# Layer 0 of a four-layer network: head values in 31 orthonormal coordinates with the denominator as the 32nd column, and the causal mask as a product on GpSimd

## The chip, the cores and the metric

The kernel runs on one core of one Trainium2 chip. Times are device microseconds of one execution of the whole program, all four layers. A core has five engines that run their own instruction queues side by side and wait for one another through semaphores: TensorE (PE, matrix products, with its weight loads shown apart as PEld), VectorE (DVE), ScalarE (ACT), GpSimd (POOL), and SyncE (SP), which here only issues DMAs. Matrix products end in PSUM, which is used here in eight banks of 128 lanes by 512 words; the other tiles lie in SBUF.

## The reference, cut to what matters

The network has four layers, each of the form x + layer(group_norm(x)). Only layer 0 is touched. It works on 16 images of 192 channels and 32 x 32 pixels, read as 1024 tokens. Its core is an mLSTM with 12 heads of 32 dimensions:

```
def step(carry, inp):
    ...
    C_new = f_s[..., None] * Cst + i_s[..., None] * (vt[..., :, None] * kt[..., None, :])
    n_new = f_s * nst + i_s * kt
    denom = jnp.maximum(jnp.abs(jnp.einsum('bhd,bhd->bh', n_new, qt)), 1.0)[..., None]
    h = jnp.einsum('bhde,bhe->bhd', C_new, qt) / denom
...
mu = hs.mean(-1, keepdims=True)
var = hs.var(-1, keepdims=True)
hn = ((hs - mu) / jnp.sqrt(var + 1e-05)).reshape(bsz, s, INNER) * mh_w + mh_b
h_out = (hn + skip * x_act) * jax.nn.silu(z)
return seq + (h_out @ w_down + b_down)
```

The result of that block and silu(seq @ w_lin + b_lin) are added, and a 3 x 3 convolution, a batch norm and a leaky ReLU follow. In the kernel the scan is done in chunks of 128 tokens: inside a chunk every token looks at the earlier ones through a matrix of scores, and a state per head carries what lies before the chunk.

One identity matters for the change. A head's output is normalized over its 32 dimensions, so its mean is taken away at once, and what is left lies in a space of 31 dimensions. With numerator u (mean already removed) and denominator e, the normalized head is u / sqrt(mean(u^2) + 1e-5 * max(e^2, 1)); the division by the denominator never has to be made.

## The kernel before

**Stages of an image.** `layer0` (line 153 on) handles one image at a time in `image(b, conv)`: image 0 first, then images 1 to 15 in a device loop (line 735) whose end is a barrier over all engines (`L735` in the profile). An image has three stages.

- *Head:* group norm, channel norm, the projections to `x_in` and the gate `sz`, a short causal convolution to `xact`, the gates and their running sums, the projections `qT` and `kT`, and `qs`, the queries scaled by the state's decay (six matmuls of `L547` whose results are multiplied on VectorE by `L551`, one PSUM bank each).
- *Chunks:* eight chunks of 128 tokens. Twelve calls of `scores(n)` each make the score tiles for two pairs (chunk, group of four heads); `turned(c)` turns a chunk's values and keys so that tokens lie on the lanes; `finish(c)` makes a chunk's outputs and updates the state.
- *Tail:* `w_lin` and `w_down`, the sum with the input copy `xr`, and the writes into the padded image `ypad`, from which the 3 x 3 convolution reads.

The convolution of image b - 1 is a generator, `conv3`, of 45 steps of one tap each (three PSUM passes of 15 taps, each pass ended by ScalarE's copy `yo`, `L392`). `fill(n)` draws n steps from it and puts them between other TensorE work. In image 0 there is nothing to draw from. In the chunk stage the order of instructions on each engine is the order of the program (`tc.manual_schedule()`); elsewhere a scheduler orders them, and it may place matmuls of the tail between the last chunks.

**The lines the change touches.**

- `scores`: for each of four PSUM banks a matmul of the identity with `mask` in bfloat16 (`L608`) first writes 0 or -1e30; then the gate exponents are added (`itg`, `at`), and beside them the products of keys and queries are made (both `L613`). ScalarE takes the exponential of the first half (`L619`), VectorE multiplies it with the second (`L622`), which gives `D`.
- `turned`: values times `cent` (`L584`), a matrix that takes away each head's mean, copied by ScalarE to `va` (`L588`) with 33 columns a head, the last of which is 1; keys transposed (`L592`) and copied to `kt`; the weighted values `vw` on GpSimd (`L596`).
- `finish`: into one PSUM bank `nd` go the numerators of three groups of four heads (`L632` from the chunk, `L645` from the state `cst`) and, as a fourth block of columns, the denominators (`L638` with `onec`, which picks a row by its place, and `L650` with `nst`, the state's denominator column). Each of these is 12 small matmuls, 32 output lanes each, four of them beside one another in the array. ScalarE squares both; GpSimd takes the maximum for the denominator (`L659`); the state is updated; two convolution taps follow; then a matmul with `mean32` (`L680`) and three with `dsel` (`L682`) make variance plus floor on every lane. Ln and Exp (`L683`, `L684`) give its inverse root, VectorE multiplies it to the numerators (`L685`), scales by `mh_w` and adds the skip path (`L687`, three times), and GpSimd multiplies by the gate into `hT` (`L691`).
- PSUM: `misc()` hands out two banks in turn, for `turned`, for the state's update and for the norm. `ps()`, used in head and tail, goes round these two and the four score banks. `nd` has one bank, the convolution another.
- Tail: outputs are 192 channels, done as two blocks of 128 lanes, the second with its 64 channels doubled (the weights hold these columns twice), so that both halves of the lanes of `ypad`'s second part get all pixels. Per block and half image two matmuls with `w_lin` and three with `w_down`, 20 in all; ScalarE applies Silu, which needs another function table than Ln and Exp.

An fp32 matmul appears in the trace as two records, so x24 stands for 12 matmuls; a transpose and the bfloat16 product appear as one.

Of the kernel before, what the change touches and what calls it, by code (L numbers as in the profile page):

```python
# [20 lines left out]
L = H * W  # L21
# [131 lines left out]
def layer0(tc, cx, NB, ydram, sdram, w1d):  # L153
    nc, I = cx.nc, cx.I
    with ExitStack() as ctx:
# [43 lines left out]
        mh_w, mh_b = (vec(nm, 128, nc.scalar) for nm in ("mh_w", "mh_b"))  # L199
# [18 lines left out]
        mask = wp.tile([128, 2 * CH], BF16, name="mask")  # L218
        identb = wp.tile([128, 128], BF16, name="identb")
        nc.vector.tensor_copy(identb, cx.ident)  # L220
# [9 lines left out]
        dsel = wp.tile([128, 3, 128], F32, name="dsel")  # L230
        idj = cx.ident.rearrange("p (j r) -> p r j", r=32)
        rowr = wp.tile([128, 3], F32, name="rowr")
        nc.vector.tensor_reduce(rowr, idj[:, 0:3, :], AX.X, ALU.add)
        for g in range(3):
            nc.vector.tensor_scalar(dsel[:, g, :], blk, rowr[:, g : g + 1], None, op0=ALU.mult)
# [12 lines left out]

        onec = wp.tile([128, 34], F32, name="onec")
        nc.vector.memset(onec, 0.0)  # L250
        nc.vector.memset(onec[:, 2:3], 1.0)
# [15 lines left out]
        mean32 = wp.tile([128, 128], F32, name="mean32")  # L267
        nc.vector.tensor_scalar(mean32, blk, 1.0 / DH, None, op0=ALU.mult)
        cent = wp.tile([128, 128], F32, name="cent")
        nc.vector.tensor_sub(cent, cx.ident, mean32)  # L270
# [6 lines left out]

        nc.vector.tensor_copy(
# [44 lines left out]
        w_down = wp.tile([128, 3, 256], F32, name="w_down")  # L323
        w_lin = wp.tile([P6, 2, 256], F32, name="w_lin")
        for t, nm, p in ((w_down, "w_down", 128), (w_lin, "w_lin", P6)):
            nc.sync.dma_start(t[:, :, 0:C], I[nm].rearrange("(k p) o -> p k o", p=p))
            nc.sync.dma_start(t[:, :, C:], I[nm][:, 128:C].rearrange("(k p) o -> p k o", p=p))
# [22 lines left out]
        for i in range(2):  # L350
            t = wp.tile([128, NH, HW1], F32, name="va%d" % i)
            nc.gpsimd.memset(t, 1.0)
            vas.append(t)

        nst = wp.tile([128, 3, DH], F32, name="nst")
        nc.gpsimd.memset(nst, 0.0)
# [44 lines left out]
        def image(b, conv):  # L401
# [166 lines left out]
            cst = big.tile([128, 3, HW1], F32, name="cst")  # L568
# [3 lines left out]
            to_den = slice(INNER, INNER + CH)  # L572
# [5 lines left out]
            def turned(c):  # L578


                cs = slice(c * CH, (c + 1) * CH)
                va, p = vas[c % 2], misc()
                for g in range(3):
                    nc.tensor.matmul(  # L584
                        p[:, groups3[g]], lhsT=x_in[:, g, 3 + c * CH : 3 + (c + 1) * CH], rhs=cent,
                        start=True, stop=True,
                    )
                nc.scalar.copy(va[:, :, 0:DH], p[:, 0:INNER].rearrange("p (h d) -> p h d", d=DH))  # L588
                if c < NCH - 1:
                    p = misc()  # L590
                    for g in range(3):
# [3 lines left out]
                    vw = wk2.tile([128, NH, HW1], F32, tag="vw", name="vw")  # L595
                    nc.gpsimd.tensor_mul(  # L596
                        vw, va, gtok[:, c].unsqueeze(2).to_broadcast([128, NH, HW1]),
# [3 lines left out]
            def scores(n):  # L601
# [5 lines left out]
                for j in range(4):  # L607
                    nc.tensor.matmul(S[j][:, two], lhsT=identb, rhs=mask, start=True, stop=False)  # L608
                for l_, r_, o in ((itg, at, 0), (kT, qT, 2)):
                    for i, (c, g) in enumerate(todo):  # L610
                        cs = slice(c * CH, (c + 1) * CH)
                        for j, r in enumerate(blocks4):
                            nc.tensor.matmul(  # L613
                                S[j][:, (o + i) * CH : (o + i + 1) * CH], lhsT=l_[r, g, cs],
                                rhs=r_[r, cs] if o == 0 else r_[r, g, cs], start=False, stop=(o == 2 and i == 1),
                            )
                for j in range(4):
                    d = wk2.tile([128, 2 * CH], F32, tag="D", name="D", bufs=12)
# [3 lines left out]
                    nc.vector.tensor_mul(d, d, S[j][:, 2 * CH :])  # L622

            def finish(c):


                cs = slice(c * CH, (c + 1) * CH)
                va = vas[c % 2]
                nd = psn.tile([128, HL], F32, name="nd")
                for g in range(3):  # L630
                    for j, r in enumerate(blocks4):
                        nc.tensor.matmul(  # L632
                            nd[r, groups3[g]], lhsT=va[:, 4 * g + j, 0:DH], rhs=D[c, g, j],
                            start=(g == 0), stop=False,
                        )
# [1367 lines left out]
```

## Time and profile before

| What | Value |
|---|---|
| median of three runs | 15609.16 us (15584.52 to 15626.19) |
| the profiled execution, its own time | 15591.93 us |
| span from its first to its last instruction | 15590.1 us |
| mean granted TensorE clock | 0.838 |
| layer 0, from the start to 3335 us | 21% of the span |
| 209.8 to 3269 us: PE, DVE, ACT, POOL busy of 3059 us | 2935, 1326, 1166, 272 us |
| the same, granted TensorE clock | 0.98 |
| 3335 to 15590 us: PE, DVE, ACT, POOL busy of 12,255 us | 9456, 10,877, 8013, 9563 us |

The profile is one execution, taken by the hardware profiler. A line of the timeline gives start and length in us, engine, source line, operation, output <- inputs, shape and count; in brackets stands the idle time of the engine before it and the instruction that ended it. The granted clock is the share of full speed at which the clock of TensorE was let through. A row of the stage table gives the busy time of each engine in a stretch with its instructions in brackets. Matmuls overlap in the array and their ends are modelled, so the distance between two starts says more than a length. In layers 1 to 3 VectorE and GpSimd are the busy engines; in layer 0 it is TensorE.

### The profile page before, as it was taken

The page shows a single profiled execution, that of the slowest core. Times are in us where ns is not written, and L with a number is a line of the kernel's source. Part 1 is how long each engine was busy: PE and PEld are TensorE (multiplying, and loading weights), DVE is VectorE, ACT ScalarE, POOL GpSimd, SP SyncE. Part 2 cuts the span into 40 slices and gives each one's busy share as a digit, 9 for nine tenths or more (in the row PEclk, how much of TensorE's full clock was granted, in tenths as well). Part 3 has the DMA queues.
Part 4 walks back from the last instruction along what each step waited for, and adds up shares of the span by engine and source line. Part 5 has one row for each costly group of instructions (what it writes and reads, how often), then busy time and mean ns, then how long its engine had stood idle before and what let it go on. Part 6 is the DMA issues. An engine that isn't in the chain of part 4 may idle for free. (4 is left out here: it accounts for less than half of the span.)

```text
span 15590.1 us, 196674 instructions
## 1 busy us (share of the span) xinstructions
PE 12621.5 (81%) x72384; PEld 5045.6 (32%) x72384; DVE 12310.8 (79%) x10295; ACT 9263.9 (59%) x12084; POOL 9861.8 (63%) x5787
## 2 busy tenths in 40 slices
PE   9999999987787777877787777877787777878755
PEld 5555555542222222222222222222222222222212
DVE  4444444448988999999989898898989898988997
ACT  3333333326666666666666666666666666666665
POOL 1000000006787878787878787878878787878785
PEclk9999999997787888878788888887888887878766
DMA  1000000017777787878787878787777787777775
GB/s 29 12 15 14 15 14 15 15 40 189 201 195 200 188 207 188 210 182 214 182 211 183 213 184 211 183 210 189 202 194 198 194 202 195 199 195 193 201 182 129
DMA packets 852126, 2412.70 MB, mean 155 GB/s; under 512 B 114352, under 2 KB 234240, under 8 KB 843520
## 3 DMA queue, kind: packets, MB, share of 16 engines
q1 hardware_dynamic: 838496, 2397.64, 60.2%
q8 instruction: 580, 9.50, 0.3%
q10 hardware_dynamic: 12704, 2.72, 0.1%
q14 instruction: 346, 2.83, 0.1%
HBM read 2018.92 MB, written 364.30 MB: 153 GB/s over the span
## 5 line engine op out<-in xcount | busy, mean ns | idle before, releaser
L1863 POOL TENSOR_TENSOR hc<-h,cb 128x1024 f32<-128x1024 f32 x3072 | 7247.3, 2371 | 2046.2 <-DVE h L1851 1557.8
L1851 DVE TENSOR_TENSOR_SCAN h<-dA,xt 128x1024 f32<-128x1024 f32 x3072 | 6912.8, 2273 | 297.0 <-POOL hc L1863 289.1
L1842 DVE TENSOR_TENSOR xt<-xt,bb 128x1024 f32<-128x1024 f32 x3072 | 3633.4, 1227 | 852.7 <-ACT xt L1831 718.9
L1835 ACT ACTIVATE dA<-dl,A 128x1024 f32<-128x1024 f32 x3072 | 3506.7, 1146 | 801.2 <-DMA dl<-dld 672.8
L1893 PE MATMUL acc<-hc,sel 128*32 128x256 f32 x24576 | 2406.8, 473 | 1707.6 <-POOL hc L1863 1705.0
L782 PE MATMUL mm<-pad,dg 128*128 128x512 f32 (+1 forms) x5580 | 2899.3, 655 | 13.3 <-ACT pad L782 9.9
L1831 ACT COPY xt<-du 128x1024 f32<-128x1024 f32 x1536 | 1557.6, 1014 | 1361.7 <-DVE h L1851 1183.5
L1893 PEld LDWEIGHTS acc<-hc,sel 128*32 128x32 f32 x24576 | 562.2, 120 | 4055.4 <-POOL hc L1863 2897.2
L782 PEld LDWEIGHTS mm<-pad,dg 128*128 128x128 f32 (+1 forms) x5580 | 995.5, 192 | 1479.2 <-issue 1363.3
L596 POOL TENSOR_TENSOR vw<-va,gtok 128x396 f32<-128x396 f32 x112 | 95.2, 850 | 1712.0 <-ACT va L588 1712.0
L782 PE MATMUL mm<-x,wgt 96*128 96x512 f32 (+1 forms) x1664 | 1064.5, 775 | 140.1 <-ACT o L782 50.0
L1884 PE MATMUL acc<-y,ident 128*128 128x512 f32 x576 | 445.7, 866 | 445.5 <-ACT y L1903 444.5
L782 POOL TENSOR_TENSOR t<-x 96x768 f32<-96x768 f32 (+4 forms) x510 | 647.5, 1290 | 204.6 <-PE mm L782 204.2
L691 POOL TENSOR_TENSOR x_in<-x_in,sz 128x384 f32<-128x384 f32 x128 | 116.8, 913 | 750.5 <-DVE x_in L687 676.7
L782 PE MATMUL mm<-d,xT 128*96 128x256 f32 x2048 | 569.1, 416 | 5.6 <-ACT o L782 5.3
L782 PEld LDWEIGHTS mm<-x,wgt 96*128 96x128 f32 (+1 forms) x1664 | 342.1, 226 | 669.9 <-issue 364.5
L782 POOL TENSOR_TENSOR duh<-dlh,xx 128x512 f32<-128x512 f32 x384 | 537.5, 1400 | 30.1
L782 POOL TENSOR_TENSOR dlh<-dlh,e 128x512 f32<-128x512 f32 x384 | 488.4, 1272 | 103.1 <-ACT e L782 101.2
L782 PE MATMUL mm<-xd,dtw 12*128 12x512 f32 x768 | 534.5, 782 | 10.0 <-ACT z L782 10.0
L622 DVE TENSOR_TENSOR D<-D,s 128x256 f32<-128x256 f32 x768 | 270.8, 415 | 322.6 <-ACT D L619 322.6
L389 PE MATMUL pc<-ypad,w_c 128*64 128x512 f32 (+1 forms) x1152 | 442.9, 633 | 80.4 <-PEq L735 41.3
L619 ACT ACTIVATE D<-s 128x256 f32<-128x256 f32 x768 | 232.7, 390 | 426.3 <-PE s L613 426.3
(331 smaller groups left out, 15374.9 us busy)
## 6 DMA issues: line engine op xcount, KB each, us to landing
dl<-dld SPq DMA_DIRECT2D x1536, 512.0 KB
du<-dud SPq DMA_DIRECT2D x1536, 512.0 KB
dld<-dlh SPq DMA_DIRECT2D x384, 256.0 KB
dud<-duh SPq DMA_DIRECT2D x384, 256.0 KB
bb<-xdr SPq DMA_DIRECT2D x128, 512.0 KB
cb<-xdr SPq DMA_DIRECT2D x128, 512.0 KB
dg<-dqd SPq DMA_DIRECT2D x270, 192.0 KB
zd<-z SPq DMA_DIRECT2D x48, 512.0 KB
```

The lines of the kernel that those rows point to most:

```text
L389: nc.tensor.matmul(p[r, :], lhsT=w_, rhs=v, start=(n == 0), stop=(n == 14))
L619: nc.scalar.activation(d, S[j][:, two], AF.Exp)
L622: nc.vector.tensor_mul(d, d, S[j][:, 2 * CH :])
L691: nc.gpsimd.tensor_mul(hT[:, :, cs], hT[:, :, cs], sz[:, :, cs])
L782: return f(out, *args, **kw)
L1831: self.nc.scalar.copy(self.xt[n], self.du[n])
L1835: self.nc.scalar.activation(self.dA[u % 3], self.dl[n % 2], AF.Exp, scale=self.A[:, blk, n : n + 1])
L1842: self.nc.vector.tensor_mul(self.xt[(n + 1 + blk) % 2], self.xt[n % 2], self.bb[blk])
L1851: nc.vector.tensor_tensor_scan(*views, 0.0, op0=ALU.mult, op1=ALU.add)
L1863: self.nc.gpsimd.tensor_mul(*views)
L1884: nc.tensor.matmul(acc, lhsT=self.cx.ident, rhs=self.y[:, g, half(pair)], start=True, stop=False)
L1893: nc.tensor.matmul(self.acc[rows4(q), q4(s)], lhsT=self.sel[:, m, :], rhs=self.hc[u % 3][:, q4(q)], start=False, stop=(s + m + blk == 3),)
```

## The change

The values of a head are no longer centred but turned into 31 orthonormal coordinates of the space without the mean (`to31`, a Helmert matrix per head, whose 32nd column is zero). The 32nd column of `va` is left at 1, so that numerator and denominator come out of one set of matmuls, and `cst` carries both. `onec`, `nst`, `dsel` and their matmuls go. A VectorE instruction raises the square of row 31 to at least 1 (`last` is 1 there and 0 elsewhere), and `norm32` weighs the coordinates with 1/32 and row 31 with 1e-5. A new step `leave(c)`, called one iteration later, goes back to channels with `back` (the transposed matrix times `mh_w`), adds the skip path from PSUM and applies the gate. The mask becomes a tile of ones and zeros in fp32 that GpSimd multiplies to `D`, after VectorE has capped the exponential at 2 in the instruction that multiplies it with the keys' products. `D` gets 14 buffers in place of 12.

In the tail the second block of channels is made once, its two half images side by side in the two halves of the lanes; two DMAs in a new function `both()`, at the start of the next iteration, copy each half to the other lanes of `ypad`. Taps are drawn in other places: `fill(2)` where `fill(3)` stood, and one and eight steps ahead of the last two `leave` calls.

```diff
-        mask = wp.tile([128, 2 * CH], BF16, name="mask")
...
+        mask = wp.tile([128, 2 * CH], F32, name="mask")
...
             def scores(n):
...
-                for j in range(4):
-                    nc.tensor.matmul(S[j][:, two], lhsT=identb, rhs=mask, start=True, stop=False)
...
-                    d = wk2.tile([128, 2 * CH], F32, tag="D", name="D", bufs=12)
+                    d = wk2.tile([128, 2 * CH], F32, tag="D", name="D", bufs=14)
...
-                    nc.vector.tensor_mul(d, d, S[j][:, 2 * CH :])
+                    nc.vector.scalar_tensor_tensor(
+                        d, d, 2.0, S[j][:, 2 * CH :], op0=ALU.min, op1=ALU.mult
+                    )
+                    nc.gpsimd.tensor_mul(d, d, mask)
...
             def finish(c):
...
-                for g in range(3):
-                    for j, r in enumerate(blocks4):
-                        nc.tensor.matmul(
-                            nd[r, to_den], lhsT=onec[:, 2 - g : 34 - g], rhs=D[c, g, j],
-                            start=False, stop=(c == 0 and g == 2),
-                        )
...
-                    for g in range(3):
-                        for r in blocks4:
-                            nc.tensor.matmul(
-                                nd[r, to_den], lhsT=nst[r, g, :], rhs=qs[r, g, cs], start=False, stop=(g == 2)
-                            )
...
-                nc.scalar.activation(h2, nd[:, 0:INNER], AF.Square)
-                dd = wk2.tile([128, CH], F32, tag="dd", name="dd")
-                nc.scalar.activation(dd, nd[:, to_den], AF.Square, scale=1e-5**0.5)
-                nc.gpsimd.tensor_scalar(dd, dd, 1e-5, None, op0=ALU.max)
+                nc.scalar.activation(h2, nd, AF.Square)
+                nc.vector.tensor_scalar(h2, h2, last, None, op0=ALU.max)
...
                 fill(2)
-                p = misc()
-                nc.tensor.matmul(p[:, 0:INNER], lhsT=mean32, rhs=h2, start=True, stop=False)
-                for g in range(3):
-                    nc.tensor.matmul(p[:, groups3[g]], lhsT=dsel[:, g, :], rhs=dd, start=False, stop=(g == 2))
...
+                p = misc()[:, 0:INNER]
+                nc.tensor.matmul(p, lhsT=norm32, rhs=h2, start=True, stop=True)
+                nc.scalar.activation(h2, p, AF.Ln)
+                nc.scalar.activation(h2, h2, AF.Exp, scale=-0.5)
+                nc.vector.tensor_mul(h2, h2, nd)
+                normed.append((c, h2))
+
+            def leave():
+
+                c, h2 = normed.pop()
+                cs = slice(c * CH, (c + 1) * CH)
+                p = misc()[:, 0:INNER]
                 for g in range(3):
-                    nc.vector.scalar_tensor_tensor(
-                        hT[:, g, cs], h2[:, groups3[g]], mh_w[:, g : g + 1], xact[:, g, cs],
-                        op0=ALU.mult, op1=ALU.add,
-                    )
+                    nc.tensor.matmul(
+                        p[:, groups3[g]], lhsT=back[:, g, :], rhs=h2[:, groups3[g]], start=True, stop=True
+                    )
+                nc.vector.tensor_add(hT[:, :, cs], xact[:, :, cs], p.rearrange("p (g t) -> p g t", g=3))
                 nc.gpsimd.tensor_mul(hT[:, :, cs], hT[:, :, cs], sz[:, :, cs])
...
                         turned(begun)
                         begun += 1
+                    if normed:
+                        leave()
...
                     else:
-                        fill(3)
+                        fill(2)
+                fill(1)
+                leave()
                 finish(ready)
+                fill(8)
+                leave()
...
+            for n in range(3):
+                e = n // 2
+                parts = [(n, slice(0, 128), slice(0, 128))] if n < 2 else [
+                    (0, slice(128, C), lower), (1, slice(128, C), upper)
+                ]
+                pl, pd = ps(), ps()
+                for p, w_, v, k in ((pl, w_lin, xn, 2), (pd, w_down, hT, 3)):
+                    for i in range(k):
+                        for hf, o, r in parts:
+                            nc.tensor.matmul(
+                                p[r, :], lhsT=w_[:, i, o], rhs=v[:, i, half(hf)], start=(i == 0), stop=(i == k - 1)
+                            )
...
+        def both():
+
+            lower, upper = slice(0, 64), slice(64, 128)
+            nc.sync.dma_start(ypad[upper, 1, 1:17, 0:W], ypad[lower, 1, 1:17, 1 : 1 + W])
+            nc.sync.dma_start(ypad[lower, 1, 17:33, 1 : 1 + W], ypad[upper, 1, 17:33, 0:W])
...
         with tc.For_i(1, NB, 1) as b:
+            both()
             image(b, conv3(b - 1))
+        both()
```

## The prediction

> **What bounds the kernel now.** I read the busy shares by slice first, then the stages of one image, then the instructions of one chunk, then the tail. The chain that ended last covers only the last few per cent of the span and says nothing of layer 0. The edit touches layer 0 alone, and layer 0 is over by 3335 us; the remaining 12,255 us of layers 1 to 3 issue the same instructions in the same order on every engine, so I count them as unchanged. Layer 0 is sixteen images, fifteen in a loop with a period of 203.98 us (the first `L389` matmul of two iterations starts at 826.72 and 1030.70). Its stages, in the columns us, PE, PEld, DVE, ACT, POOL, granted clock, DMA share, GB/s:
>
> ```profile
> 826.72:911.00 84.28, 84.23 (x228) 36.11 (x229) 46.21 (x70) 33.35 (x42) 0.00 (x0) 0.98 0.04 10
> 911.00:1008.31 97.31, 93.71 (x1547) 62.82 (x1547) 33.45 (x95) 34.41 (x96) 17.27 (x29) 1.00 0.06 18
> 1008.31:1030.70 22.39, 17.59 (x38) 7.07 (x37) 9.10 (x16) 10.27 (x12) 0.91 (x1) 0.92 0.06 13
> ```
>
> The middle row is the chunk stage, the one that is rewritten. TensorE is busy 93.71 of 97.31 us, VectorE and ScalarE a third of it, GpSimd less than a fifth. A busy share of matmuls alone proves little, since their ends are modelled, so I look at starts. One finished chunk and the scores behind it:
>
> ```profile
> 956.97 0.86 PE L632 MATMUL nd<-D,va 128*32 128x128 f32 x24
> 957.65 0.84 PE L638 MATMUL nd<-D,onec 128*32 128x128 f32 x24
> 958.42 0.86 PE L645 MATMUL nd<-qs,cst 32*32 32x128 f32 x24
> 959.10 0.83 PE L650 MATMUL nd<-qs,nst 32*32 32x128 f32 x24
> 959.86 0.40 PE L666 MATMUL ps<-vw,kt 128*32 128x33 f32 x24
> ...
> 963.15 0.91 PE L680 MATMUL ps<-h,mean 128*128 128x384 f32 x2
> 963.90 0.83 PE L682 MATMUL ps<-dd,dsel 128*128 128x128 f32 x6
> 964.57 0.60 PE L608 MATMUL s<-mask,identb 128*128 128x256 bf16 x4
> 965.10 0.73 PE L613 MATMUL s<-at,itg 32*128 32x128 f32 x16
> ...
> 966.20 0.94 PE L584 MATMUL ps<-cent,x_in 128*128 128x128 f32 x6
> ```
>
> Each group starts where the last one stops issuing, with no wait named. The price of a group is therefore the distance to the next start, and PE time taken out is taken out of the image until another wait appears.
>
> **What goes.** *Mask matmuls:* 964.57 to 965.10, 0.53 us, twelve times an image. The first of them hides under a wait: the six `qs` products on VectorE end at 912.74 and free the score banks only then (first `L613` at 913.00). In the new order one convolution tap of 0.86 us, which filled that wait, is issued earlier in the head; the products move back by it, and scores start 0.67 us later instead of earlier. So 11 x 0.53 - 0.67 = **5.2**. *Denominator matmuls:* `va` to `kt` is 959.86 - 956.97 = 2.89 with four groups; with `va` and `cst` alone it is 0.77 + 0.76 (one change of tile shape stays behind each), so 1.36 for seven chunks and 0.67 for the first: **10.2**. *`dsel`:* 0.67 x 8 = **5.4**. *Tail projections:* before, 20 matmuls of 512 columns at 0.86 (the spacing of the `w_q` matmuls is 2.57 for three) = 17.2. After, ten of these and five pairs of 64-column halves. The convolution already runs such pairs: eight records, two pairs, in 1.87 us, so 0.93 a pair. 17.2 - 8.6 - 4.65 = **4.0** (between 4.3 if a pair costs one, and 0 if the halves don't overlap; the row speaks for the first).
>
> *The wait in the tail:*
>
> ```profile
> 1011.75 5.32 PE L39 MATMUL ps<-x_in,w_down 128*128 128x512 f32 x12
> ...
> 1016.91 1.88 PE L39 MATMUL ps<-xn,w_lin 96*128 96x512 f32 x4
> ...
> 1020.65 7.11 PE L39 MATMUL ps<-x_in,w_down 128*128 128x512 f32 x12 [1.86 <-POOL x_in L691]
> ...
> 1030.70 2.63 PE L389 MATMUL pc<-ypad,w_c 128*128 128x512 f32 x4 [2.94 <-PEq L735]
> ```
>
> PE idles 1.86 us for the last gating product, and the same twelve records then take 7.11 instead of 5.32: the granted clock is down. Before, the last Ln and Exp of the chunk each stand behind a Silu with a table load of 1.28. After, they come ahead of all three Silus, with three pairs of taps (2.8 us) over them, and behind the last `back` matmuls lie six projections (5.2 us) over an add and a gate (0.26 + 0.55 + 0.91, with handovers 1.9). Wait and slow stretch go: 1.86 + 1.75 = **3.6**. What is late next is the loop's end (2.94 idle), where the last two `ypad` writes and the barrier stay as they were. Sum of what goes: **28.4 us an image**.
>
> **What comes.** *`back` matmuls:* three a chunk, between `dsel` (0.67) and `cent` (0.77); 0.70 x 8 = **5.6**. *A new wait in `leave`:* PE runs in order, scores, `turned`, `leave`. `leave` takes the PSUM buffer that `turned` used for the values (two buffers, turn about), so it waits until ScalarE has copied them out, and that copy stands behind four exponentials:
>
> ```profile
> 932.90 1.21 ACT L619 ACTIVATE D<-s 128x256 f32<-128x256 f32 x4 [0.41 <-PE s L613]
> 933.97 0.52 ACT L588 COPY va<-ps 128x384 f32<-128x384 f32 x1
> ```
>
> Counted from the end of the norm matmul (before: of `dsel`): Ln from 0.26, Exp to 1.30, exponentials from about 1.2, the copy from 1.07 later to 2.8. PE has issued scores (1.1) and `turned` (1.10) by 2.2. Waiting behind it in PE's queue is the whole of `finish`. I take 0.7 at the five iterations that have both steps with a transpose (n = 3, 4, 6, 7, 9), and 0.35 for the last two `leave`s, which wait for Exp and product: **3.9** (bounds: nothing, if the copy slips ahead; 1.0 each, if VectorE's product is later). *The first scores:* PE now idles from 910.7 to 913.7 without the mask matmuls in between. The Trainium skill ("TensorE: Matmul & The Clock Gate", Part 1) has the clock fall to half after an idle window of some 3.4 us; by it a gap of 2.98 need not cost anything. The row above says that 1.86 was enough for 1.75 us. By the rule 0, by the row 1.75; the gap of 2.94 at the loop's end was followed by a granted clock of 0.72 to 1.00 over the next 12 us, so I take **1.0**. Sum of what comes: **10.5 us**.
>
> **What I cost at nothing, and its cover.** *Mask on GpSimd:* 48 products of 128x256. A later layer has the same shape on the same engine:
>
> ```profile
> L782 POOL TENSOR_TENSOR d<-ident,e 128x256 f32<-128x256 f32 x384 | 235.0, 620 | 74.0 <-PE mm L782 72.6 <-POOL d L782 0.4
> ```
>
> 0.62 us each (235.0 us over 384; 620 is the mean in ns). GpSimd then has 48 x 0.62 + 15 x 0.9 = 43 us in a stage of some 75 (gates of 0.913 and weightings of 0.85, `L691` and `L596`, make the 15). The skill ("GPSIMD Engine Reference", 8. Key points) advises against it: elementwise work is about twice as fast on VectorE. The row agrees on the price (VectorE's four `L622` products take 1.41, 0.35 each), and following the rule would put 17 us on VectorE and not 30 on GpSimd. Neither is on PE's path, so rule and change give the same sum. The latency counts more. Between scores and the `finish` that reads them PE has at the tightest (n = 1 to 2) `turned` 1.10, two taps 1.72, scores 1.1 and eight matmuls, 4.4 in all; exponential, product and four masks take 0.96 + 4 x 0.62 = 3.4. The cover holds to 0.85 us a mask. *VectorE:* the products become three-operand ones (0.35 to 0.49 each, `L687` and `L729` by their columns: up to 7 us more), the maximum of 128x384 is new (0.3 by `L433`, 0.55 by `L685`), three 0.29 us `L687` become one add of 0.55; all in 33 of 75 us. The maximum lies between Square and norm matmul: 0.26 + 0.49 + 0.55 + 0.15 = 1.45 against 0.33 + 1.87 of `kt` and taps. *The two `ypad` copies:* 2,048 packets of 128 bytes on SP's queue, ahead of the load of the next input, which is not due for an image. No such copy is in the trace; the small packets of queue 10 took 0.02 us of an engine each, so some 3 us on sixteen, and the taps that read the copied half start 13.3 us into the iteration. Upper end: a few us. *Setup:* two constants and a broadcast more, four loads and some products less, all due after 100 us.
>
> **Sum.** 28.4 - 10.5 = 17.9 us an image, 268 for fifteen. Image 0 has no taps to lie over its waits (it already shows 0.28 before each norm matmul); I take 11. Together 279 us. The profiled execution, 15591.93 (span 15590.1), becomes 15313; the runs' median 15609.16 lies 17 above it, so **15330**.
>
> **Rivals.** *More comes out* (chance 0.15): `leave` doesn't wait, the clock stays up, a pair costs one tap. 17.9 + 3.9 + 1.0 + 0.4 = 23 an image, 15240. For it: PE's queue shows no such wait now. Against it: the two-buffer order. *The chain of a chunk becomes the bound* (0.18): Ln, Exp, product, `back`, add, gate now span two iterations; if every chunk loses another 1 us on it, 17.9 - 8 = 10 an image, 15450. For it: VectorE's product already stopped PE once an image (0.16 at 1003.00). Against it: ScalarE and VectorE are under half busy. *GpSimd becomes the bound, and the kernel slower* (0.05): all masks and gates of an image on one engine. With 13 us of other work it equals the old stage plus what the tail gains when 13 + 48p = 97.3 + 7.6, p = 1.91 us; at 2.2 us, with VectorE in its way, each image loses 14, 15830. Against it: 0.62 by the row, and VectorE's 128x1024 products take 1.227 beside a GpSimd that is 78% busy in layer 2 and 1.22 beside an idle one in layer 0. *The change doesn't do what it says* (0.02): PE is paced by something the starts don't show; time as before, 15609.
>
> **From cases to numbers.** The forecast, 14 to 21 us an image, has 0.60 (15280 to 15390). About 0.3% (47 us, 3 us an image) can be told from no change. The range takes the whole forecast, most of the first rival and the near half of the second: 15235 to 15450. Faster 0.92, same 0.03, slower 0.05.
>
> **What would show it.** Period about 186 us; no `L608`, `onec`, `nst`, `dsel` rows; `va` to `kt` 1.5 us; `back` 0.7 with some 0.7 idle before it, released by ScalarE's `va` copy; no idle before the last `w_down`; a 3 us gap before the first scores; GpSimd's masks near 0.62. The forecast is wrong if `nd` matmuls wait for GpSimd, if layers 1 to 3 (12,255 us) change length, or if the loop's end grows beyond 2.94.

## The result and the profile after

| | before | after | after / before |
|---|---|---|---|
| median of the runs | 15599.7 us (4: 15584.52 to 15626.19) | 15412.83 us (4: 15383.76 to 15424.77) | 0.9866 [0.9854, 0.9878] |
| the profiled execution | 15591.93 us | 15416.19 us | |
| of it, layer 0 | 3326.2 us | 3090.7 us | |
| of it, layers 1 to 3 | 12,263.9 us | 12,323.7 us | |
| mean period of the image loop | 204.85 us | 189.70 us | |

Layer 0 is counted here, in every kernel, up to the start of its last convolution tap, and layers 1 to 3 from there to the end of the span; the prediction cut at 3335 us, a little later. The change is faster, as forecast, and the time lies in the range of 15235 to 15450, though not in the forecast's own 15280 to 15390: 187 us came out and not 279. For the profiled execution the forecast was 15313; the 103 us above it are 43 in layer 0 (235.5 gained, 279 forecast) and 60 in layers 1 to 3, where nothing was to change.

The stages of one image, read as before (head, chunks, tail), and below them a stretch of the chunk stage alone; columns us, PE, PEld, DVE, ACT, POOL, granted clock, DMA share, GB/s:

```profile
775.62:863.45 87.83, 85.53 (x229) 36.76 (x229) 47.52 (x72) 33.46 (x42) 0.00 (x0) 0.97 0.06 12
863.45:951.17 87.72, 83.42 (x1138) 50.74 (x1138) 36.29 (x87) 34.27 (x90) 45.54 (x62) 0.94 0.05 17
951.17:966.47 15.30, 12.34 (x41) 4.57 (x39) 6.29 (x10) 3.47 (x6) 0.91 (x1) 0.99 0.09 19
863.45:873.20 9.75, 8.59 (x45) 5.23 (x45) 2.70 (x6) 2.85 (x7) 3.56 (x5) 0.51 0.08 29
```

The chunk stage has 409 TensorE records fewer and is 10 us shorter, but its clock fell from 1.00 to 0.94, and the last row shows where: its first 9.75 us had half the clock. GpSimd is busy for 45.54 us of it; TensorE waits for its masks for 0.3 us in all of layer 0 (below). The tail went from 22.39 to 15.30 us.

TensorE's timeline at the first scores of that image, behind the six matmuls for `qs` (`L549`, below called the spread matmuls):

```profile
859.15 1.99 PE L549 MATMUL ps<-isc,sel 32*128 32x512 f32 x12
863.45 1.62 PE L613 MATMUL s<-at,itg 32*128 32x128 f32 x13 [2.30 <-DVE qs L553]
...
866.06 1.65 PE L584 MATMUL ps<-to,x_in 128*128 128x128 f32 x6
...
869.51 3.78 PE L391 MATMUL pc<-ypad,w_c 128*128 128x512 f32 x4 [1.16 <-ACT yo L394]
...
874.60 0.94 PE L584 MATMUL ps<-to,x_in 128*128 128x128 f32 x6
875.37 0.49 PE L594 MATMUL ps<-ident,kT 128*128 128x128 f32 x3
875.70 1.88 PE L391 MATMUL pc<-ypad,w_c 128*128 128x512 f32 x4
```

TensorE idles 2.30 us for the `qs` products, and then the same six `turned` records take 1.65 and not 0.94, the same two taps 3.78 and not 1.88. Before, a tap lay in this wait and the `turned` records behind it took 0.94:

```profile
907.91 1.99 PE L547 MATMUL ps<-isc,sel 32*128 32x512 f32 x12
909.83 1.12 PE L389 MATMUL pc<-ypad,w_c2p 64*128 64x512 f32 x2
911.00 0.27 PE L608 MATMUL s<-mask,identb 128*128 128x256 bf16 x1
...
914.10 0.94 PE L584 MATMUL ps<-cent,x_in 128*128 128x128 f32 x6
```

The records of the granted clock know two values, 0.5 and 1, and half rate comes in pieces of 3.41, 6.83 or 10.24 us, that is one, two or three steps of a grid of 3.41 us. The steps around the first scores of the changed kernel's image (same columns as the stages):

```profile
860.20:863.61 3.41, 1.11 (x10) 0.28 (x5) 3.30 (x6) 0.00 (x0) 0.00 (x0) 1.00 0.00 0
863.61:867.02 3.41, 3.41 (x36) 2.96 (x37) 1.21 (x4) 1.24 (x4) 0.26 (x1) 0.50 0.02 5
867.02:870.44 3.42, 2.26 (x8) 1.43 (x7) 1.33 (x3) 1.61 (x4) 3.31 (x5) 0.50 0.02 7
870.44:873.85 3.41, 3.41 (x16) 1.31 (x18) 0.00 (x0) 0.00 (x0) 0.00 (x0) 0.50 0.18 70
873.85:877.26 3.41, 3.41 (x41) 2.30 (x37) 1.42 (x4) 1.96 (x6) 1.58 (x3) 1.00 0.00 0
```

This image has three steps at half rate; the one before and the one after it have two, behind the same wait of 2.30 us. All fifteen images of the changed kernel have half rate here. Of the kernel before, six of fifteen have some; the image at 911.00 has none.

A chunk further on, TensorE again:

```profile
904.21 0.94 PE L683 MATMUL ps<-h,back 128*128 128x128 f32 x6 [0.51 <-ACT va L588]
905.08 0.86 PE L639 MATMUL nd<-D,va 128*32 128x128 f32 x24
905.87 0.86 PE L646 MATMUL nd<-qs,cst 32*32 32x128 f32 x24
906.66 0.40 PE L658 MATMUL ps<-vw,kt 128*32 128x32 f32 x24
```

From `va` to `kt` it is 1.58 us where it was 2.89, and ahead of `back` stands the new wait, released by ScalarE's copy as forecast. The idle times of TensorE in the groups that carry the change, summed over layer 0 (110 to 3080 us; last columns: busy us, mean ns, idle us and what ended it):

```profile
L391 PE MATMUL pc<-ypad,w_c 128*128 128x512 f32 x576 | 339.9, 723 | 61.8 <-PEq L751 41.5 <-ACT yo L394 18.1 <-DVE ypad L739 2.2
L613 PE MATMUL s<-at,itg 32*128 32x128 f32 x3072 | 156.3, 306 | 35.8 <-DVE qs L553 34.5
L683 PE MATMUL ps<-h,back 128*128 128x128 f32 x768 | 116.8, 288 | 41.4 <-ACT va L588 38.0 <-DVE h L674 3.4
L671 PE MATMUL ps<-h,norm 128*128 128x384 f32 x256 | 112.7, 522 | 6.7 <-DVE h L651 6.7
L639 PE MATMUL nd<-D,va 128*32 128x128 f32 x3072 | 111.5, 277 | 0.3 <-POOL D L627 0.3
```

The mask on GpSimd makes TensorE wait 0.3 us in all of layer 0. `L613` idles 34.5 us over fifteen images, 2.3 each; what it costs in clock doesn't stand in this column.

### The profile page after: what moved, and what is told of

It reads as the page before. It is cut to its first block, busy times and chain, and to the rows that moved or that the text cites. A ratio compares the mean times of both kernels' runs of the same rounds, so it can differ in the third digit from the quotient of the medians.

```text
span 15414.4 us, 184312 instructions
## 1 busy us (share of the span) xinstructions
PE 12384.4 (80%) x65856; PEld 4810.3 (31%) x65856; DVE 12329.6 (80%) x10115; ACT 9160.4 (59%) x11881; POOL 10313.5 (67%) x6314
## 4 chain that ended last, share of the span: by engine, by line
PE 19%; DVE 16%; POOL 14%; issue 13%; DMA 10%; ACT 7%; SPq 1%; DVEq 0%; POOLq 0%; ACTq 0%
PE mm L800 15%; DVE h L1869 10%; POOL hc L1881 9%; DVE xt L1860 5%; DMA dl<-dld 3%; PE acc L1911 3%; DMA du<-dud 2%; POOL t L800 2%; ACT dA L1853 2%; ACT xt L1849 2%; DMA y<-ydram 1%; DMA yh<-yd 1%; POOL dlh L800 1%; PE acc L1902 1%; DMA yd<-y 1%
## 5 line engine op out<-in xcount | busy, mean ns | idle before, releaser
L627 POOL TENSOR_TENSOR D<-D,mask 128x256 f32<-128x256 f32 x768 | 542.7, 738 | 2101.1 <-DVE D L624 2101.1
L391 PE MATMUL pc<-ypad,w_c 128*64 128x512 f32 (+1 forms) x1152 | 480.3, 664 | 74.2 <-PEq L751 41.5
L624 DVE SCALAR_TENSOR_TENSOR D<-D,s 128x256 f32<-128x256 f32 x768 | 272.0, 416 | 255.2 <-ACT D L620 255.2
L800 PEld LDWEIGHTS mm<-d,xT 128*96 128x96 f32 x2048 | 328.0, 174 | 261.0 <-issue 164.0
```

Of the source, the lines that this page charges most:

```text
L391: nc.tensor.matmul(p[r, :], lhsT=w_, rhs=v, start=(n == 0), stop=(n == 14))
L624: nc.vector.scalar_tensor_tensor(d, d, 2.0, S[j][:, 2 * CH :], op0=ALU.min, op1=ALU.mult)
L627: nc.gpsimd.tensor_mul(d, d, mask)
L800: return f(out, *args, **kw)
```

## Experiments

Clock time lost means here, worked out from the trace: the time in a stretch, each part weighed with 1 minus its granted clock. It is an upper measure of the time it costs, since a matmul that waits for something else loses nothing by it. "Layer 0" and "image" are those of the table above; the changed kernel has 3090.7 and 189.70. Lost clock time in the 12 us from an image's first score matmul: 0.9 us before, 4.2 after, in the mean of the fifteen images. Line numbers are those of each run's own kernel.

**The wait at the first scores, filled.** First with work whose result nobody reads (e1_warm):

```diff
+                warm = psn.tile([128, HL], F32, name="nd")
+                for _ in range(5):
+                    nc.tensor.matmul(warm[:, 0:256], lhsT=cx.ident, rhs=kT[:, 0, 0:256], start=True, stop=True)
                 ready = begun = 0
```

> The changed kernel with five extra matmuls of 256 columns (0.43 us each by the 512-column rows, 2.1 us in all) put on TensorE in the wait before the first scores of an image; their result is read by nobody. Theory 'clock' (the half rate after the 2.9 us gap costs 4.2 us an image, the mean over the images in the profile): no slow stretch after the scores, period 189.7 -> about 185.5 us, total 15413 -> about 15345. Rival 'traffic' (the scores after the gap are slow for another reason, such as GpSimd and VectorE working beside them): slow stretch stays, total within 10 us of 15413. If the extra work only delays the scores, the total rises by up to 20.

15333.05 us, ratio 0.9815 [0.9801, 0.9828]; image 185.9; no clock time lost at the scores, in any of the fifteen images. Two lines of TensorE and a stretch behind the first score:

```profile
855.54 2.43 PE L694 MATMUL nd<-kT,ident 128*128 128x256 f32 x10
857.91 1.21 PE L613 MATMUL s<-at,itg 32*128 32x128 f32 x13
857.90:866.00 8.10, 6.74 (x85) 4.82 (x85) 3.03 (x8) 3.32 (x10) 3.57 (x5) 1.00 0.09 34
```

Over whole iterations the loss falls from 6.9 to 1.5 us, and the image is 3.8 us shorter: a microsecond of lost clock time is worth some 0.7 us here (an estimate from this run). Then with taps of the convolution, taken from the head and from the places behind (e2_taps):

```diff
-            fill(15)
+            fill(14)
...
                 ready = begun = 0
+                fill(3)
...
-                        fill(2)
+                        fill(2 if n else 1)
```

> The changed kernel with convolution taps drawn ahead of the first scores, in the same wait: useful work instead of extra work, and one tap fewer behind the first turn. Theory 'clock': the slow stretch goes (4.2 us an image) and so does most of the 1.2 us wait for ScalarE's yo copy behind the first turn: about 5 us an image, total about 15333. Rival 'traffic': only the wait for yo goes, 1 us an image, total about 15397.

15273.79 us, ratio 0.9778 [0.9765, 0.9792]; image 181.9; faster than expected, because the two taps in the wait no longer take 1.7 us elsewhere, the waits for `yo` shrink, and around the loop's end 1.0 us of clock time is lost and not 2.7. The scheduler still puts one of the three ahead of the spread matmuls; two lie in the wait:

```profile
837.43 1.99 PE L549 MATMUL ps<-isc,sel 32*128 32x512 f32 x12
839.36 1.99 PE L391 MATMUL pc<-ypad,w_c 128*128 128x512 f32 x4
841.73 1.20 PE L613 MATMUL s<-at,itg 32*128 32x128 f32 x13 [0.39 <-DVE qs L553]
...
843.42 0.94 PE L584 MATMUL ps<-to,x_in 128*128 128x128 f32 x6
```

The scores start no earlier behind the spread matmuls (in these two kernels as in the changed one it is 2.89 us from the last spread record to the first score), but `turned` runs at its full rate. So the time is lost to the clock, not to the wait. How much work is needed was asked twice. The first try moves only the fifteenth tap (e10_one_tap):

```diff
-            fill(15)
+            fill(14)
...
                 ready = begun = 0
+                fill(1)
```

> The changed kernel with one tap fewer drawn before the order by hand, and that one drawn at its head, between the spread matmuls and the first scores (some 1 to 2 us of TensorE's work in a wait of 2.9); nothing is added and the later taps keep their places. Theory 'the idle time before the scores is what drops the clock, and any work in it that leaves less than about 1.7 us idle keeps it': the 4.2 us an image go, image 189.7 - 4.2 = 185.5, whole about 15340. Rival 'it takes a full gap of work': the scores and turned still run at half rate for part of the 8 us, image 187.5 to 189, whole 15370 to 15395.

15380.17 us, ratio 0.9854 [0.9839, 0.9869]. The scheduler drew that tap ahead again, so TensorE's order is that of the changed kernel, and the theories aren't told apart; it serves as another measurement of the changed kernel. The second leaves `fill(15)`, puts `fill(1)` at the head of the order by hand and takes the tap from behind the first `turned` (e11_half_gap):

> The changed kernel with one conv tap moved from behind the first turned to ahead of the first scores: in this one place of an image one tap (1.0 us of TensorE's work) now lies in the wait of 2.9 us, and no instruction is added or removed. Between the changed kernel (nothing in the wait, 4.2 us an image lost to half rate behind it, image 189.7) and e2_taps (two taps, nothing lost, image 181.9). Theory 'the idle time that is left decides': 1.3 to 1.9 us are left, no more than the idle time of the kernel before, which lost 0.9 there: image 189.7 - 4.2 + 0 to 0.9 - 1.0 for the tap itself = 184.5 to 185.5, whole about 15330. Rival 'the clock falls by the share of the last microseconds that was busy, and one tap is too little': half of the loss stays, image 187 or more, whole 15365 or more.

15309.81 us, ratio 0.9809 [0.9795, 0.9822]; image 184.3, near the first theory's 184.5 to 185.5. TensorE:

```profile
842.57 1.13 PE L391 MATMUL pc<-ypad,w_c 128*128 128x512 f32 x2
844.94 1.42 PE L613 MATMUL s<-at,itg 32*128 32x128 f32 x13 [1.24 <-DVE qs L553]
...
847.36 1.65 PE L584 MATMUL ps<-to,x_in 128*128 128x128 f32 x6
848.80 0.69 PE L594 MATMUL ps<-ident,kT 128*128 128x128 f32 x3
849.33 1.02 PE L391 MATMUL pc<-ypad,w_c 128*128 128x512 f32 x2
```

With 1.24 us idle the clock is still halved, but for one step of 3.41 us, and in eleven of the fifteen images: 1.3 us an image are lost in place of 4.2. That is more than the 0 to 0.9 of the first theory, so its number held better than its reason.

**The mask back on TensorE** (e3_mask_pe). All else as changed; the GpSimd product goes, the bfloat16 matmul and the mask of 0 and -1e30 return:

```diff
+                for j in range(4):
+                    nc.tensor.matmul(S[j][:, two], lhsT=identb, rhs=mask, start=True, stop=False)
...
-                    nc.vector.scalar_tensor_tensor(
-                        d, d, 2.0, S[j][:, 2 * CH :], op0=ALU.min, op1=ALU.mult
-                    )
-                    nc.gpsimd.tensor_mul(d, d, mask)
+                    nc.vector.tensor_mul(d, d, S[j][:, 2 * CH :])
```

> The changed kernel with the mask back on TensorE (bfloat16 identity times 0 or -1e30, VectorE's plain product, no GpSimd product): one part of the change undone. By the forecast this part is worth 5.2 us less 1.0 for the clock, so undoing it should cost 4.2 us an image, total about 15480. Theory 'clock': the mask matmuls keep the clock up in the gap (0.9 us lost after the scores before the change, 4.2 after it), so undoing it costs 11 x 0.53 = 5.8 and gives back 3.3: 2.5 us an image, total about 15453. If GpSimd's masks delay the chunk too, less than that.

15429.17 us, ratio 0.9879 [0.9864, 0.9894]; layer 0 3167.1, that is 76 us more or 4.8 an image. The median of the whole lies only 39 us above that of all twelve runs of the changed order (15390.6, below), so the 76 are those of the profiled execution. In one of the theories the mask matmuls hold the clock up, too. They don't:

```profile
874.62 1.99 PE L550 MATMUL ps<-isc,sel 32*128 32x512 f32 x12
878.90 0.37 PE L611 MATMUL s<-mask,identb 128*128 128x256 bf16 x1 [2.30 <-DVE qs L554]
879.50 0.80 PE L611 MATMUL s<-mask,identb 128*128 128x256 bf16 x3 [0.23 <-DVE qs L554]
```

They need the same PSUM banks as the scores and so come behind the same 2.30 us; 4.7 us an image are lost in the 12 us from the first of them, no less than the 4.2 of the changed kernel.

**The mask on VectorE** (e7_mask_dve). The rule that its expectation names is the one that the prediction takes from the skill.

```diff
-                    nc.gpsimd.tensor_mul(d, d, mask)
+                    nc.vector.tensor_mul(d, d, mask)
```

> The changed kernel with the mask product on VectorE instead of GpSimd. The rule that elementwise work belongs on VectorE would make this faster; the forecast holds that neither engine is on TensorE's path, so the total stays within 15 us of the changed kernel (VectorE gets 48 products of 0.34 us more an image and is then busy for about 60 of some 80 us in the chunk stage). If VectorE's queue becomes late for the score banks, the total rises by up to 1 us an iteration, 190 us.

15457.02 us, ratio 0.9893 [0.9878, 0.9908]; layer 0 3170.7, 80 us more. The same group lines of this kernel (110 to 3160 us), TensorE's norm matmul and the new VectorE product:

```profile
L671 PE MATMUL ps<-h,norm 128*128 128x384 f32 x256 | 114.4, 529 | 41.5 <-DVE h L651 41.5
L627 DVE TENSOR_TENSOR D<-D,mask 128x256 f32<-128x256 f32 x768 | 386.1, 503 | 26.3
```

A product takes 0.50 us on VectorE and not the 0.34 expected. VectorE is still idle for a third of the chunk stage (59.8 of 94.1 us busy in the one from 895.9 on), but the maximum `L651`, which the norm matmul waits for, now stands behind products in its queue, and TensorE's wait for it goes from 6.7 to 41.5 us. That is 35 of the 80 us. Clock time lost in layer 0 rises from 110.9 to 134.8 us, which places up to 24 more; the rest is not placed. The mask as a product pays because TensorE hardly waits for GpSimd's queue (0.3 us in layer 0).

**The wait in `leave`** (e6_leave). On top of e2_taps, the two taps that stood behind `leave` go ahead of it; where `finish` follows, one tap does, and `finish` draws one fewer:

```diff
+                    out = 2 * n >= 3 * ready + 3
+                    late = bool(normed)
+                    if not out:
+                        fill(2 if n else 1)
+                    elif late:
+                        fill(1)
                     if normed:
                         leave()
...
-                        finish(ready)
+                        finish(ready, 1 if late else 2)
```

> The kernel with taps in the gap (15274 us), and besides that taps drawn between turn and leave instead of behind leave, so that they lie over leave's wait for ScalarE's copy of the values (0.45 to 0.51 us, five times an image). Theory 'the wait is PE time': 5 x 0.47 = 2.4 us an image less, minus some 0.2 us three times where only one tap is left over the Square and the maximum: about 1.8 us an image, total about 15245. Rival 'the wait only moves' (Ln, Exp, product and add bound the chunk): within 8 us of 15274.

15260.74 us, ratio 0.9777 [0.9764, 0.979]; layer 0 only 3.4 us less than e2_taps: the rival held, though the totals, from two chips, differ by 13 us (their ratios by 0.0001). TensorE's groups in layer 0 (110 to 2960 us):

```profile
L391 PE MATMUL pc<-ypad,w_c 128*64 128x512 f32 x540 | 135.8, 609 | 21.2 <-ACT yo L394 21.2
...
L683 PE MATMUL ps<-h,back 128*128 128x128 f32 x768 | 114.9, 286 | 5.8 <-DVE h L674 3.4 <-ACT va L588 2.4
```

The wait for the copy fell from 38.0 to 2.4 us, but a wait for `yo` of 21 us came in its place at the convolution's passes, and 1.1 us an image more (17 us) was lost to the clock around the loop's end. This is the fastest kernel in the study, by no more than its runs vary from those of e2_taps.

**The tail, undone** (e8_tail). The tail is as before (20 matmuls of 512 columns, four writes, no `both()`); the rest is as changed.

> The changed kernel with the tail's projections as before (second block of channels made for both lane halves, 20 matmuls of 512 columns, no copies between images). Forecast: pairs of 64-column halves save 4.0 us an image, so undoing them costs about 64 us, total about 15477. Rival 'halves don't overlap': no change. If the new order of the tail also depended on it, up to 3.6 us an image more, about 15535.

15387.65 us, ratio 0.9862 [0.9846, 0.9878]; layer 0 3091.6, image 189.8: no change at all where 64 us were expected, or up to 122. TensorE at the first scores:

```profile
855.26 1.99 PE L550 MATMUL ps<-isc,sel 32*128 32x512 f32 x12
857.19 1.12 PE L392 MATMUL pc<-ypad,w_c2p 64*128 64x512 f32 x2
858.36 2.39 PE L614 MATMUL s<-at,itg 32*128 32x128 f32 x15
```

The fifteenth tap is back between the spread matmuls and the scores, as in the kernel before. So it was the rewritten tail, in the same scheduled region, with which that tap moved ahead. Here 1.8 us an image are lost at the scores and 0.1 at the loop's start, where the changed kernel loses 4.2 and 2.4; the slower tail takes back what this gives.

This run also shows that the recorded idle time does not decide alone. The first scores come in 0.6 us apart as their banks get free, and the profile counts no idle stretch over 0.12 us in the step of 3.41 us ahead of half rate. Yet eight of the fifteen images, this one too, have two steps of it:

```profile
858.32:861.73 3.41, 3.03 (x36) 2.33 (x37) 1.96 (x4) 0.59 (x3) 0.00 (x0) 1.00 0.02 5
861.73:868.56 6.83, 5.67 (x19) 2.74 (x22) 1.93 (x5) 2.15 (x6) 3.56 (x5) 0.50 0.10 38
```

To see the tail at an equal clock, it was undone on e2_taps as well (e9_taps_tail):

> e2_taps with the whole tail as before (four passes, 256-column weights). Undoing the tail alone cost nothing: its image took 189.8 us against 189.7. Theory 'the clock covered it': there the scheduler left a tap between the spread matmuls and the first scores, and by the clock of the slices that kernel lost 1.9 us an image to half rate where the changed kernel lost 6.9; net of that the pairs are worth some 5 us an image. With the taps placed by hand in both, the clock is the same, and the tail's worth must show: image 181.9 + 4 to 5 = 186 to 187, layer 0 +60 to +75 us against e2_taps, the whole about 15340. Rival 'the pairs are worth nothing' (their matmuls are hidden behind the residual's DMA or the elementwise chain of the tail): image 182, whole 15274.

15307.85 us, ratio 0.981 [0.9796, 0.9823]; layer 0 3038.6 against 2976.2, or 62.4 us in fifteen images: 4.2 each. The scheduler left all three taps behind the spread matmuls here, with a wait of 0.78 us for `yo` among them; but `turned` starts at the same place in the image, to 0.1 us, and no clock time is lost at the scores in either kernel, so nearly all of the 4.2 is the tail. The first theory holds for layer 0; the whole came out 30 us lower than it said, with layers 1 to 3 at 12,266.6 (e2_taps: 12,295.8).

**Layers 1 to 3.** The changed kernel has more inputs, so two unused constants were added to the kernel before (e4_before_inputs), and the changed kernel was run again as it is (e5_again):

```diff
+        "c_extra1": np.eye(128, dtype=f),
+        "c_extra2": np.eye(128, dtype=f),
```

> The kernel before with two more input arrays of 128x128 that nothing reads, as the changed kernel has two more: layers 1 to 3 took 12263 us before and 12323 after, with the same instructions in the same order at the same on-chip places. If the place of the inputs in device memory makes that difference, the total rises from 15600 by 40 to 60. If it is chance or something else, the total stays within 20 of 15600.

> The changed kernel once more, unchanged, to split its time again. Layers 1 to 3 took 12264 us in the profile before, 12324 in that after, and 12286 to 12296 in the experiments derived from the changed kernel. Theory 'chance': these layers vary from run to run by some 20 us whatever layer 0 does; here about 12290, layer 0 about 3091 to its last tap, ratio to the kernel before about 0.985. Theory 'the changed kernel slows layers 1 to 3': 12316 to 12324 again, ratio 0.9866.

The first took 15616.04 us, ratio 1.0 [0.9992, 1.0008]: the inputs do nothing. The second took 15392.08, ratio 0.9858 [0.9843, 0.9873], layer 0 3091.4, layers 1 to 3 12,302.4. Together with e10_one_tap the same order of work was profiled three times: layer 0 was 3090.6 to 3091.4, layers 1 to 3 12,323.7, 12,302.4 and 12,279.3. Over all profiles here the latter lie between 12,263.9 and 12,323.7, with identical instruction order, and the kernel before had the shortest. Its profiled execution also lies 22 us below the median of all 48 runs of it (15613.8); with its layer 0 taken off, that median leaves 12,286 for layers 1 to 3. The twelve runs of the changed order have a median of 15390.6, which leaves 12,298. So most of the 60 us is which executions were profiled; whether some 10 us belong to the change stays open. The runs come from several chips (e5_again and e10_one_tap from two), so chip and execution are not told apart. One pattern in the profiles speaks for the change: the four kernels with the old tail have the four shortest layers 1 to 3 (12,263.9 to 12,272.9). The medians, less layer 0 as above, don't bear it out: e4_before_inputs leaves 12,292 and e3_mask_pe, with the new tail, 12,260.

## Why the prediction was right, and where it was short

The mechanism held: TensorE paces layer 0, and what is taken from its queue comes out of the image. The terms, per image:

| term | forecast | measured | by what |
|---|---|---|---|
| mask matmuls | 5.2 | 4.8 | e3_mask_pe, 76.4 / 16; the 0.67 that the forecast took off for the tap is not in it |
| denominator matmuls | 10.2 | 9.8 | 7 x (2.89 - 1.58), and 0.67 for the first |
| `dsel` | 5.4 | not run alone | its rows are gone |
| tail projections | 4.0 | 4.2 | e9_taps_tail against e2_taps |
| tail wait and slow stretch | 3.6 | 2.9 | the wait of 1.86 is gone; clock lost in the last 24 us of the loop 1.37 to 0.30 |
| `back` | -5.6 | -6.6 | eight spacings of 0.76 to 0.87 |
| wait in `leave` | -3.9 | -2.6 | 41.4 / 16, `L683` |
| clock at first scores | -1.0 | -3.3 | 4.2 against 0.9 lost |
| clock after the loop's end | 0 | -0.5 | 2.38 against 1.93 lost |

With 5.4 for `dsel` the measured column sums to 14.1; the loop gained 15.15, forecast 17.9. Some 0.4 of the rest are shorter waits for `yo` (37.0 to 30.6 us in layer 0). The clock rows are upper measures: at the 0.7 of e1_warm the last two would be -2.6 and the sum 15.3, by that estimate. The 3.9 for the wait in `leave` has the 0.35 once for both last `leave`s.

**The term that failed** is "by the rule 0, by the row 1.75 ... so I take 1.0" for the clock at the first scores. The gap itself was forecast (2.98; from start to start it is 2.89, of which the profile counts 2.30 as idle), and so was the tap that leaves it. What I took from the tail's row was only its stretch of twelve records, which ended at the loop's barrier; the row could not show how long half rate lasts. Behind 2.30 us it lasted 6.83 and 10.24 us in turn and took 4.2 us of clock time, some 3 to 4 us of the image by e1_warm, above both of my ends. The trace before had a better measure than the row: behind its loop's end, after 2.94 us idle, 1.9 us are lost in the mean. I had read the idle window of some 3.4 us in the Trainium skill ("TensorE: Matmul & The Clock Gate", Part 1) as the least length of an idle stretch that costs anything, which gave nothing for this gap. The steps of 3.41 us in the clock's records agree with the window's length; the measurement decides against that use of it. e1_warm, e2_taps and e11_half_gap show the cause: with work in the wait, and the scores no earlier behind the spread matmuls, the loss goes.

**Layers 1 to 3 "unchanged"** was right in the order of instructions; a change of their length was one of the forecast's own signs of being wrong. Their length differs by up to 60 us from one execution to the next, which the 17 us between the profiled execution and the median did not cover. Of the 83 us between 15330 and 15412.83, 43 are layer 0, and 22 the distance of these four runs from the twelve of the same order.

**Right by size:** the period's parts above, no wait for GpSimd, no idle time before the last `w_down`, the loop's end at 2.96 (2.94 before). **Right in place, wrong in size:** the new wait, 0.45 to 0.51 at the five iterations named, not 0.7; in return three `back` matmuls cost up to 0.87, not 0.70. **GpSimd's product** takes longer than its row promised, with cover to spare; the page of the profile:

```profile
L627 POOL TENSOR_TENSOR D<-D,mask 128x256 f32<-128x256 f32 x768 | 542.7, 738 | 2101.1 <-DVE D L624 2101.1
```

0.738 us and not 0.62; the cover was said to hold to 0.85. **Wrong:** "rule and change give the same sum" for the mask on VectorE. Following the Trainium skill ("GPSIMD Engine Reference", 8. Key points) costs 80 us of layer 0 here. I had compared busy times and not what stands behind the products in VectorE's queue. The price was off, too: VectorE's product of two SBUF tiles takes 503 ns against 738 on GpSimd, so it is 1.5 times as fast and not twice, and the `L622` row with which I agreed reads one operand from PSUM. **Image 0 and the setup** gave 8 us (235.5 less 15 x 15.15), not 11: the norm matmuls wait 6.7 us for the maximum, where those before waited 1.8.

Of the rivals, "the chain of a chunk becomes the bound" did not come about: its new waits cost less than the forecast had for them. The result lies near its 15450 for another reason.

## What to carry to other kernels

When an edit takes work off TensorE, look at each idle stretch of TensorE that is left, ahead of matmuls that set the pace: a wait of 2.30 us cost more in clock behind it here than it lasted, and useful work moved into it paid, though the matmuls behind it started no earlier. An edit in one place of a scheduled region can move an instruction in another, so compare the order of every engine, and judge the parts of an edit at an equal clock, or two effects of opposite sign pass for none. An engine's idle share does not say that a new instruction on it is free; look at what the critical engine waits for in that queue.

## What the hardware showed unexpectedly

- Half rate behind short waits of TensorE, in steps of 3.41 us: two or three steps after 2.30 us idle, one step in eleven of fifteen images after 1.24 us, none after 0.39 us (e2_taps), but two steps in eight of fifteen images of e8_tail with pauses of no more than 0.12 us. So the length of one idle stretch does not decide alone; what does is not shown.
- Periods of the changed kernel's loop alternate between 190.5 and 188.35 us with the same instructions: in one, 1.3 us of clock time are lost in the 30 us after the group norm's first matmul and 5.1 at the scores, in the next 0 and 3.4. Two periods are 378.88 us, which is 111 steps of 3.413 us: the loop meets the grid of the clock at the same two places again and again. So one profiled image can mislead; take the mean of several.
- VectorE's maximum `L651` takes 663 ns in the mean beside GpSimd's masks, and 417 and 419 without them (e7_mask_dve and e3_mask_pe), while the product `L624`, which reads PSUM, takes 416 and, in e7_mask_dve, 414. Within the changed kernel, the 16 maxima with no GpSimd instruction beside them took 419 to 421 ns, the other 112 took 459 to 955. So it is the work on GpSimd beside it that slows the maximum. The Trainium skill ("GPSIMD Engine Reference", 1. Specifications) has the two engines share their SBUF interfaces and names contention for VectorE instructions in a two-port mode or with two SBUF inputs; this would fit, but whether the maximum is one of these no run here shows.
